# Four adjacency layers on one core: where last-pass norms sit inside a score step, a first map split in two, and where layer 1's first weights lie

## The chip, the cores and the metric

The kernel runs on one core of one Trainium2 chip. The metric is the device time of one execution in microseconds (us), less being better. A core has TensorE (PE, matrix products and transposes into PSUM), VectorE (DVE), ScalarE (ACT), GpSimd (POOL) and SyncE (SP, which here issues DMAs). Each engine takes its own instructions in order and waits on semaphores for the others.

## The reference

The input x is 128 batches x 64 nodes x 256 channels, adj is 64 x 64, all float32. Four layers follow each other, each of the form `x = layernorm(x + layer(x))`.

```
layer 0: two graph convolutions relu(adj @ (h W + b)), then LSTMs over windows of 1, 2, 3 and 4 nodes
layer 1: agg = A_hat @ x;  h = relu(batchnorm(agg W1.T + b1));  out = batchnorm(h W2.T + b2)
layer 2: Xq = x W_lin.T;  Xv = x W_val.T                 (4 heads)
         e[edge, head] = a . leaky_relu(Xq[src] + Xq[dst], 0.2) + log(adj[src, dst])
         attn = softmax of e over the edges of one src;   Y = sum over edges of attn * Xv[dst];   Y W_out.T
layer 3: U = eigenvectors of the normalized Laplacian of adj;  U relu((U.T x) W1 + b1) W2 + b2
```

The change touches the start of layer 1 and the place where layer 1's end and layer 2's beginning run side by side.

## The kernel before

The activations stay in one SBUF tile `X` of 128 partitions x 64 tiles x 256 channels (two batches per tile). The tile framework reorders what the source issues: it lists each engine's instructions by its own costs, so the order on an engine is not the order of the source. Where the source forces an order it does so by hand: `in_order(eng, on)` keeps what is issued inside it behind the last instruction of that engine so far, and `after(ins, those)` adds a dependency.

**Layer 1, first pass** (lines 1735 to 1753). Over 16 blocks `q` of four tiles: store the block (`xd`, an SP DMA), aggregate on PE (L1742), copy to `at` on ACT (L1744), multiply by `w1` (L1748, 8 matmuls), take statistics on DVE (`st1`, L1749) and copy out on ACT (L1750). Pieces of an eigenvalue solver (`pump`) run on DVE beside it. `w1` is loaded by an SP DMA (L1703) into a tile of pool `la`, which closes after this pass and lies above pool `lw`, in which `w2`, `vec1`, `vec2` and `st1` lie at the bottom of that side of memory. What a tile's memory held before decides how early it can be filled: here it is memory of layer 0's LSTM.

**Layer 1, second pass** multiplies by `w2` (L1796) and leaves the result in `Y` with statistics; then scale and shift of the second batchnorm are worked out.

**The last pass of layer 1** (`last_pass`) is a generator of 32 halves `h`, two tiles each, with two stops per half. In the first, PE transposes `y` (L1836) and DVE adds the result to `X` (L1234) and takes row statistics (L1237, L1238), all inside `ln.add`. In the second, ACT makes the next `y` (L1827, two instructions) and, for some `h`, `ln.flush` works out `1/sqrt` (DVE L1212, ACT L1214, DVE L1215 to L1218, L1249) and ACT normalizes each tile of the group (L1253). The condition `h % 2 or not h` flushes h = 0, h = 1, and then pairs {2,3}, {4,5} and so on to {30,31}.

**Layer 2's scores** (`scores`) go over 32 pairs of tiles `k`. `transposed(k)` transposes a pair (PE L1919, DVE copy L1921 to `xT`); `maps(k)` multiplies it by the query and value weights side by side, 512 columns in one PSUM bank per tile (L1930), ACT copies the first 256 columns to `xq` (L1932) and the others to `xv` (L1933), and SP stores `xv`. A step has two halves `c`: four score products `l` (L1956, traced as eight records), four copies to `xs` on ACT (L1963), four leaky relus on DVE (L1964), and the products `sc` of the half before (L1907). After `c = 0` comes `maps(k + 1)`, after `c = 1` comes `transposed(k + 2)`. The source makes the products `l` of a half wait for all ACT copies issued since the last half (the list `taken`), which includes the two `xq` copies of `maps`. PSUM tiles for `transposed`, `maps` and the last pass come from one pool of two banks (tag `m`); `xs` has six buffers.

**How they interleave.** `beside[0]` is the last pass, and every half of a score step calls `next(beside[0])` twice. So a step `k` takes two halves of the last pass, h = 3 + 2k in its first half and h = 4 + 2k in its second. Steps 0 to 14 run that way; later ones run with layer 2's softmax and values.

On the engines PE's order in a step is: maps, transposes of an even `y`, `l` (c = 1), `sc`, transposes of X, transposes of an odd `y`, `l` (c = 0 of the next step), `sc`, maps. Each `y` stands just ahead of an `l`.

Of the kernel before, what the change touches and what calls it, by code (L numbers as in the profile page):

```python
# [7 lines left out]
F32 = mybir.dt.float32  # L8
# [8 lines left out]
D = 256  # L17
P = 128
# [1241 lines left out]
def tile_adj_resnorm(ctx: ExitStack, tc: tile.TileContext, I: dict, out: bass.AP, layers: int = 4):  # L1260
    nc = tc.nc
    v, s, te = nc.vector, nc.scalar, nc.tensor
# [13 lines left out]
    kio = lambda w: w.rearrange("(k p) f -> p k f", p=P)  # L1276
# [202 lines left out]
    with tc.tile_pool(name="lw", bufs=1) as lw, tc.tile_pool(  # L1479
        name="l0c", bufs=1  # L1480
    ) as lc, tc.tile_pool(name="l0p", bufs=2, space=PSUM) as pp, tc.tile_pool(
        name="l0r", bufs=1, space=PSUM
# [27 lines left out]
        ps = pp.tile([P, 512], F32, tag="ps", name="ps")  # L1510
# [4 lines left out]
        ps = pp.tile([P, 512], F32, tag="ps", name="ps")  # L1515
        te.matmul(ps[:, :1], bda, ones[:, 0:1], start=True, stop=True)
        v.tensor_copy(rs, ps[:, :1])
        ps = pp.tile([P, 512], F32, tag="ps", name="ps")
# [4 lines left out]
        ln = Norm(nc, hn, X, 8)  # L1523
# [166 lines left out]
    lw, sm = own2(only1, name="l1w", bufs=1), own2(only1, name="l1s", bufs=2)  # L1690
    pass1 = ExitStack()
    la = own2(pass1, name="l1a", bufs=2)
    pp = own1(only1, name="l1p", bufs=7, space=PSUM)

    def lload(name, shape, src, eng=nc.sync):
        t = lw.tile(shape, F32, tag=name, name=name)
        eng.dma_start(t, src)
        return t

    NQ = NT // 4  # L1700
    Y = [ly.tile([P, 2, 512], F32, tag=f"Y{q}", name="Y") for q in range(NQ)]
    w1 = la.tile([P, 2, 512], F32, tag="w1", name="w1", bufs=1)
    nc.sync.dma_start(w1, kio(I["W1T"]))  # L1703
    w2 = lload("w2", [P, 4, D], kio(I["W2T"]))
    vec1 = lload("vec1", [P, 3, 4], I["vec1"], s)
    vec2 = lload("vec2", [P, 3, 2], I["vec2"], s)
    st1 = lw.tile([P, 4, NQ, 6], F32, tag="st1", name="st1")
    st2 = lw.tile([P, 2, NQ, 6], F32, tag="st2", name="st2")
    xd = [dram.tile([P, 4, D], F32, tag=f"xd{q}", name=f"xd{q}") for q in range(NQ)]

# [17 lines left out]
    def xq(q):  # L1728
        return X[:, q * 4 : q * 4 + 4, :]

    def first(q, c):

        return Y[q][:, c, :] if c < 2 else xq(q).rearrange("p j d -> p (j d)")[:, (c - 2) * 512 : (c - 1) * 512]

    back = residual(NT // TG - 1, H, pp, "ps")
    for q in range(NQ):
        nc.sync.dma_start(xd[q], xq(q))
        at = la.tile([P, 2, 512], F32, tag="at", name="at")
        for k in range(2):
            ps = pp.tile([P, 512], F32, tag="ps", name="ps")  # L1740
            for j in range(4):
                te.matmul(ps[:, j * P : (j + 1) * P], X[:, q * 4 + j, k * P : (k + 1) * P], bdah,  # L1742
                          start=True, stop=True)
            s.copy(at[:, k, :], ps)  # L1744
        for c in range(4):
            ps = pp.tile([P, 512], F32, tag="ps", name="ps")
# [40 lines left out]
    for q in range(NQ):  # L1787
        h = sm.tile([P, 4, 512], F32, tag="h", name="h")
# [24 lines left out]
    @contextmanager  # L1813
    def in_order(eng, on):

        last = next((i for i in reversed(nc.cur_bb.bb.instructions) if i.engine == eng.engine), None) if on else None
        with tc.issue_after(last) if last is not None else nullcontext():
            yield

    def last_pass():  # L1820

        ln = Norm(nc, sy, X, 8, act=True)

        def normed(h):
            y = sy.tile([P, 2, 2 * P], F32, tag="y", name="y")
            for c in range(2):
                s.activation(y[:, c, :], Y[h // 2][:, c, h % 2 * 2 * P : (h % 2 + 1) * 2 * P], AF.Identity,  # L1827
                             bias=sh2[:, c : c + 1], scale=sc2[:, c : c + 1])
            return y

        y = normed(0)
        for h in range(2 * NQ):
            ps = pp.tile([P, 512], F32, tag="m", name="m")
            for i in range(2):
                for c in range(2):
                    te.transpose(ps[:, i * D + c * P : i * D + (c + 1) * P], y[:, c, i * P : (i + 1) * P], ident)  # L1836
            ln.add(2 * h, ps, 2)
            yield
            with in_order(s, h < 4):
                if h < 2 * NQ - 1:  # L1840
                    y = normed(h + 1)
            with in_order(s, h < 4):
                if h % 2 or not h:
                    ln.flush()
            yield

# [9 lines left out]
    with ExitStack() as l2:  # L1856
# [3 lines left out]
        pp = own1(l2, name="l2p", bufs=2, space=PSUM)  # L1860
        sx = own1(scoring, name="l2x", bufs=2, side="right")
# [9 lines left out]
        wqv = lt.tile([P, 2, 2 * D], F32, tag="wqv", name="wqv")  # L1871
# [16 lines left out]
        taken, late = [], []  # L1888
        beside = [iter(())]
        es, soft = [[], []], []  # L1890

        def after(ins, those, how=mybir.DependencyClass.Sync):
            for i in those:
                tc.add_manual_dep(ins.ins, i.ins.name, mybir.DependencyInfo(how, mybir.DependencyReason.DATA),
                                  reason="together")

        def products():

            k, c, xs, ready = late.pop()
            half, u_ = divmod(k, HU)  # L1900
            if u_ == 0 and c == 0:
                sc[half] = [pc.tile([P, 512], F32, tag="sc", name="sc") for _ in range(2)]
            mms = []
            for b in range(2):
                for i in range(2):
                    q = 32 * (2 * b + i)
                    mms.append(te.matmul(sc[half][c][q : q + 32, :], az[:, c, HU - 1 - u_ : 3 * HU - 1 - u_],  # L1907
                                         xs[b, i], start=(u_ == 0), stop=(u_ == HU - 1)))
            after(mms[0], ready)
            if u_ == HU - 1 and c == 1:  # L1910
                next(soft[half])
            return mms[0]

        def transposed(k):

            ps = pp.tile([P, 512], F32, tag="m", name="m")
            for i in range(2):
                for c in range(2):
                    te.transpose(ps[:, i * D + c * P : i * D + (c + 1) * P], X[:, 2 * k + i, c * P : (c + 1) * P], ident)  # L1919
            xT = sx.tile([P, 2, 2, P], F32, tag="xT", name="xT", bufs=1)  # L1920
            v.tensor_copy(xT.rearrange("p i c n -> p (i c n)"), ps)  # L1921
            return xT

        def maps(k, xT):

            xq, xv = [], sx.tile([P, 2, D], F32, tag="xv", name="xv")
            for i in range(2):
                ps = pp.tile([P, 512], F32, tag="m", name="m")
                for c in range(2):
                    te.matmul(ps, xT[:, i, c, :], wqv[:, c, :], start=(c == 0), stop=(c == 1))  # L1930
                xq.append(sx.tile([P, D], F32, tag="xq", name="xq", bufs=4))
                taken.append(s.copy(xq[i], ps[:, :D]))  # L1932
                s.copy(xv[:, i, :], ps[:, D:])  # L1933
            nc.sync.dma_start(xvd[k], xv)
            return xq

        def scores():


            K = NT // 2  # L1940
            xT = transposed(0)
            xq = maps(0, xT)
            next(beside[0])
            xT = transposed(1)
            next(beside[0])


            four = [(b, i) for i in range(2) for b in range(2)]
            for k in range(K):
                xn = None  # L1950
                for c in range(2):
                    xs, pl = {}, [pg.tile([P, 2, 512], F32, tag="l", name="l") for _ in range(2)]
                    mms = []
                    for b, i in four:
                        r = slice(b * N, (b + 1) * N)
                        mms.append(te.matmul(pl[i][:, b, :], xq[i][r, c * P : (c + 1) * P], GG[r, :], start=True, stop=True))  # L1956
                    after(mms[0], taken)
                    del taken[:]
                    next(beside[0], None)
                    ready = []  # L1960
                    for b, i in four:
                        x = xs[b, i] = sx.tile([P, E], F32, tag="xs", name="xs", bufs=6)
                        taken.append(s.copy(x, pl[i][:, b, :]))  # L1963
                        ready.append(v.scalar_tensor_tensor(x, x, 0.2, x, ALU.mult, ALU.max))  # L1964
                    if late:
                        after(products(), mms[-1:], mybir.DependencyClass.NoSync)
                    late.append((k, c, xs, ready))
                    if c == 0 and k < K - 1:
                        xn = maps(k + 1, xT)
                    if c == 1 and k < K - 2:  # L1970
                        xT = transposed(k + 2)
                    next(beside[0], None)
                xq = xn
                if k == K - 1:
                    products()
                yield
# [98 lines left out]
        lw, sm = own1(valuing, name="l2w", bufs=1), own1(valuing, name="l2s", bufs=2)  # L2075
        ln = Norm(nc, sm, X, 4, act=True)
# [16 lines left out]
        with tc.tile_pool(name="l3w", bufs=1) as l3w, tc.tile_pool(name="l3s", bufs=2) as s3, tc.tile_pool(  # L2093
            name="l3p", bufs=6, space=PSUM
        ) as p3:
            bank = lambda: p3.tile([P, 512], F32, tag="ps", name="ps")
            w1 = l3w.tile([P, 2, P], F32, tag="w31", name="w31")
# [23 lines left out]
            ag, h, uh = {}, {}, {}  # L2121
# [117 lines left out]
```

## Time and profile before

| what | value |
|---|---|
| median of 3 runs | 2429.41 us (2428.41 to 2432.4) |
| the profiled execution's own time | 2431.46 us |
| its span, first to last instruction | 2429.7 us |
| busy share of the span: PE, DVE, ACT | 94%, 75%, 40% |
| from 1515 to 1671 us (first pass of layer 1) | PE busy 149.12 of 156 |
| from 1901.15 to 1913.67 us (one score step with last-pass work) | 12.52 long, PE busy 11.06, DVE 9.53, ACT 9.49 |
| from 2067.27 to 2077.46 us (one score step without it) | 10.19 long, PE busy 10.17 |

The profile shows one execution. "Idle before" is the time in which an engine had nothing, and the name behind the arrow is what ended that. PEclk is the share of TensorE's full clock that was granted. A row such as `PE L1956 MATMUL l<-edge_s,xq ... x8` is eight merged records of source line 1956 that write `l` and read `edge_s` and `xq`; the first two numbers are start and length in us.

### The profile page before, as it was taken

The page shows a single profiled execution, that of the slowest core. Times are in us where ns is not written, and L with a number is a line of the kernel's source. Part 1 is how long each engine was busy: PE and PEld are TensorE (multiplying, and loading weights), DVE is VectorE, ACT ScalarE, POOL GpSimd, SP SyncE. Part 2 cuts the span into 40 slices and gives each one's busy share as a digit, 9 for nine tenths or more (in the row PEclk, how much of TensorE's full clock was granted, in tenths as well). Part 3 has the DMA queues.
Part 4 walks back from the last instruction along what each step waited for, and adds up shares of the span by engine and source line. Part 5 has one row for each costly group of instructions (what it writes and reads, how often), then busy time and mean ns, then how long its engine had stood idle before and what let it go on. Part 6 is the DMA issues. An engine that isn't in the chain of part 4 may idle for free. (4 is left out here: it accounts for less than half of the span.)

```text
span 2429.7 us, 29499 instructions
## 1 busy us (share of the span) xinstructions
PE 2289.1 (94%) x9016; PEld 1225.0 (50%) x9016; DVE 1817.8 (75%) x8355; ACT 974.1 (40%) x1751; POOL 77.4 (3%) x118
## 2 busy tenths in 40 slices
PE   7999999999999999999999999999988889899797
PEld 5544654444564544665444644554433333246786
DVE  4666766677887888878888888687957778457577
ACT  2333222242333243332333222334437765456575
POOL 0000000000000000000000000000000000002331
PEclk9999999999999999999999999999989999999899
DMA  6000000100100000100001000012210000511622
GB/s 216 18 18 35 1 35 1 35 18 18 53 1 35 35 18 22 49 35 1 35 35 52 1 27 1 27 49 104 78 40 27 22 22 24 98 36 48 135 88 75
DMA packets 59861, 101.26 MB, mean 42 GB/s; under 512 B 5136, under 2 KB 40080, under 8 KB 59440
## 3 DMA queue, kind: packets, MB, share of 16 engines
q1 hardware_dynamic: 54624, 88.83, 11.5%
q0 software_dynamic: 3216, 10.21, 1.4%
q8 instruction: 72, 1.18, 0.2%
q14 instruction: 93, 0.76, 0.1%
q10 hardware_dynamic: 1856, 0.28, 0.1%
HBM read 67.84 MB, written 31.46 MB: 41 GB/s over the span
## 5 line engine op out<-in xcount | busy, mean ns | idle before, releaser
L1590 PE MATMUL pq<-H,wi 128*128 128x512 f32 (+1 forms) x2016 | 836.3, 547 | 6.0 <-DVE H L1619 4.0
L1596 ACT ACTIVATE gate<-pq,bl 128x512 f32<-128x512 f32 (+1 forms) x504 | 317.3, 634 | 791.0 <-PE pq L1594 647.0
L1590 PEld LDWEIGHTS pq<-H,wi 128*128 128x128 f32 x2016 | 371.9, 191 | 330.9 <-issue 256.2
L1594 PE MATMUL pq<-lh,wh 128*128 128x512 f32 (+1 forms) x1152 | 481.8, 534 | 16.1 <-DVE lh L1614 14.4
L1594 PEld LDWEIGHTS pq<-lh,wh 128*128 128x128 f32 x1152 | 213.1, 190 | 213.4 <-issue 128.3
L1964 DVE SCALAR_TENSOR_TENSOR xs<-xs 128x512 f32<-128x512 f32 x256 | 165.2, 680 | 88.7 <-ACT xs L1963 88.2
L1956 PE MATMUL l<-edge_s,xq 64*128 64x512 f32 x512 | 135.7, 624 | 36.2 <-ACT xq L1932 19.9
L1963 ACT COPY xs<-l 128x512 f32<-128x512 f32 x256 | 136.8, 587 | 73.6 <-PE l L1956 39.0
L1612 ACT ACTIVATE gate<-lc 128x512 f32<-128x512 f32 (+1 forms) x144 | 83.5, 580 | 166.9 <-DVE lc L1608 81.1
L1930 PE MATMUL m<-wqv,xT 128*128 128x512 f32 x256 | 124.6, 624 | 0.8 <-DVE xT L1921 0.8
L1748 PE MATMUL ps<-at,w 128*128 128x512 f32 x256 | 116.9, 608 | 6.9 <-DMA w<-in_W1T_dram 5.9
L1796 PE MATMUL ps<-h,w 128*128 128x512 f32 x256 | 114.9, 607 | 4.1 <-ACT h L1790 4.1
L1253 ACT ACTIVATE X<-X,ln_sh,ln_rs 128x256 f32<-128x256 f32 x192 | 101.0, 591 | 30.7 <-DVE ln_sh L1249 24.9
L1237 DVE BATCH_NORM_STATS2 ln_st<-X 128x6 f32<-128x256 f32 x256 | 98.7, 415 | 2.3
L142 DVE COPY AQR<-eps 64x192 f32<-64x192 f32 (+1 forms) x125 | 35.0, 280 | 80.9 <-PE eps L148 80.8
L1956 PEld LDWEIGHTS l<-edge_s,xq 64*128 64x128 f32 x512 | 46.2, 188 | 88.8 <-issue 32.6
L1930 PEld LDWEIGHTS m<-wqv,xT 128*128 128x128 f32 x256 | 46.5, 195 | 78.6 <-issue 58.3
L1796 PEld LDWEIGHTS ps<-h,w 128*128 128x128 f32 x256 | 48.8, 194 | 64.0 <-issue 52.3
L1748 PEld LDWEIGHTS ps<-at,w 128*128 128x128 f32 x256 | 47.4, 193 | 62.8 <-issue 53.7
L1610 DVE TENSOR_TENSOR gate<-gate 128x512 f32<-128x512 f32 (+1 forms) x72 | 43.4, 603 | 45.7 <-ACT gate L1596 45.2
L1907 PE MATMUL sc<-xs,az 128*32 128x512 f32 x512 | 69.0, 611 | 4.6 <-DVE xs L1964 4.6
L1550 PE MATMUL ps<-wg,h 128*128 128x256 f32 x256 | 65.4, 394 | 5.9 <-DVE h L1541 5.5
(558 smaller groups left out, 3196.4 us busy)
## 6 DMA issues: line engine op xcount, KB each, us to landing
wi<-in_WihT_dram SPq DMA_DIRECT2D x16, 1024.0 KB, 4.8
wh<-in_WhhT_dram SPq DMA_DIRECT2D x12, 1024.0 KB, 6.6
X<-in_x_dram SPq DMA_DIRECT2D x16, 512.0 KB, 8.9
xd<-X SPq DMA_DIRECT2D x16, 512.0 KB, 2.6
X<-xd SPq DMA_DIRECT2D x16, 512.0 KB, 3.2
xv<-xv SPq DMA_DIRECT2D x32, 256.0 KB, 2.0
xr<-xv POOLq DMA_DIRECT2D x32, 256.0 KB, 2.9
M<-attn_d SPq DMA_DIRECT2D x16, 512.0 KB, 11.5
```

Source lines behind the costliest of these rows:

```text
L1237: nc.vector.bn_stats(st, self.X[:, k, :])
L1253: nc.scalar.activation(x, x, AF.Identity, bias=sh[:, k : k + 1], scale=rs[:, k : k + 1])
L1590: te.matmul(ps, wi[:, kk, o * P : (o + 1) * P], at(kk, k), start=(kk == 0), stop=(k == 0 and kk == 1))
L1594: te.matmul(ps, wh[:, kk, o * P : (o + 1) * P], hst[:, kk, :M], start=False, stop=(kk == 1))
L1596: s.activation(gates[gt][:, c, :M], ps, AF.Tanh if gt == 2 else AF.Sigmoid, bias=bl[:, p - 1, o : o + 1])
L1612: s.activation(g[2], cs, AF.Tanh)
L1748: te.matmul(ps, w1[:, k, c * P : (c + 1) * P], at[:, k, :], start=(k == 0), stop=(k == 1))
L1796: te.matmul(ys[c], w2[:, k, c * P : (c + 1) * P], h[:, k, :], start=(k == 2), stop=(k == 1))
L1930: te.matmul(ps, xT[:, i, c, :], wqv[:, c, :], start=(c == 0), stop=(c == 1))
L1956: mms.append(te.matmul(pl[i][:, b, :], xq[i][r, c * P : (c + 1) * P], GG[r, :], start=True, stop=True))
L1963: taken.append(s.copy(x, pl[i][:, b, :]))
L1964: ready.append(v.scalar_tensor_tensor(x, x, 0.2, x, ALU.mult, ALU.max))
```

## The change

1. `w1` moves from pool `la` to pool `lw`, as that pool's first tile, ahead of `w2`; its DMA is issued ahead of w2's. `st1` moves from `lw` to `la`.
2. In the last pass the flush condition becomes `h < 3 or h % 2 == 0 or h == 2 * NQ - 1`: h = 0, 1 and 2 alone, then {3,4}, {5,6} and so on to {29,30}, and 31 alone. For h < 3 DVE's additions and flushes are kept in order on DVE as well, and the forced order on ACT goes one half further.
3. `maps(0)` is made `apart`: the query columns of both tiles come first, each followed by its `xq` copy, and then the value columns of both.
4. The second half of h = 2 (its `normed` and flush) is issued ahead of `transposed(1)` instead of behind it.

What the two programs' instruction orders show: PE's order differs only up to step 1, where all four `l` of step 0 now stand together behind the transposes of pair 1, and two groups of `y` transposes stand behind an `l` instead of ahead of it. On ACT, in every step up to 14, before: `xq xv`, three normalizations, `xq xv`, one normalization, `y y`, `xs xs xs xs`, `y y`, `xs xs`, the square root, `xs xs`. After: `xq xv xq xv`, `y y`, `xs xs`, the square root, `xs xs`, four normalizations, `xs xs`, `y y`, `xs xs`. On SP only the two weight loads swap.

```diff
-    w1 = la.tile([P, 2, 512], F32, tag="w1", name="w1", bufs=1)
-    nc.sync.dma_start(w1, kio(I["W1T"]))
+    w1 = lload("w1", [P, 2, 512], kio(I["W1T"]))
     w2 = lload("w2", [P, 4, D], kio(I["W2T"]))
...
-    st1 = lw.tile([P, 4, NQ, 6], F32, tag="st1", name="st1")
+    st1 = la.tile([P, 4, NQ, 6], F32, tag="st1", name="st1", bufs=1)
...
-            ln.add(2 * h, ps, 2)
+            with in_order(v, h < 3):
+                ln.add(2 * h, ps, 2)
             yield
-            with in_order(s, h < 4):
+            with in_order(s, h < 5):
                 if h < 2 * NQ - 1:
                     y = normed(h + 1)
-            with in_order(s, h < 4):
-                if h % 2 or not h:
+            with in_order(s, h < 5), in_order(v, h < 3):
+                if h < 3 or h % 2 == 0 or h == 2 * NQ - 1:
                     ln.flush()
             yield
...
-        def maps(k, xT):
+        def maps(k, xT, apart=False):
 
             xq, xv = [], sx.tile([P, 2, D], F32, tag="xv", name="xv")
+            pss = [pp.tile([P, 512], F32, tag="m", name="m") for _ in range(2)]
+
+            def product(i, cols):
+                for c in range(2):
+                    te.matmul(pss[i][:, cols], xT[:, i, c, :], wqv[:, c, cols], start=(c == 0), stop=(c == 1))
+
+            def first(i):
+                xq.append(sx.tile([P, D], F32, tag="xq", name="xq", bufs=4))
+                taken.append(s.copy(xq[i], pss[i][:, :D]))
+
+            if apart:
+                for i in range(2):
+                    product(i, slice(0, D))
+                    first(i)
             for i in range(2):
-                ps = pp.tile([P, 512], F32, tag="m", name="m")
-                for c in range(2):
-                    te.matmul(ps, xT[:, i, c, :], wqv[:, c, :], start=(c == 0), stop=(c == 1))
-                xq.append(sx.tile([P, D], F32, tag="xq", name="xq", bufs=4))
-                taken.append(s.copy(xq[i], ps[:, :D]))
-                s.copy(xv[:, i, :], ps[:, D:])
+                product(i, slice(D, 2 * D) if apart else slice(0, 2 * D))
+                if not apart:
+                    first(i)
+                s.copy(xv[:, i, :], pss[i][:, D:])
             nc.sync.dma_start(xvd[k], xv)
             return xq
...
             xT = transposed(0)
-            xq = maps(0, xT)
+            xq = maps(0, xT, True)
+            next(beside[0])
             next(beside[0])
             xT = transposed(1)
-            next(beside[0])
```

## The prediction

> **What bounds the kernel now.** The page comes first: PE is busy for 94% of the span, and the rows of its products say which stretches have idle time. Then the timeline of PE alone over two score steps, the same of ACT, the timeline around the first product with `w1`, and the busy times of windows.
>
> ```profile
> PE 2289.1 (94%) x9016; PEld 1225.0 (50%) x9016; DVE 1817.8 (75%) x8355; ACT 974.1 (40%) x1751; POOL 77.4 (3%) x118
> L1956 PE MATMUL l<-edge_s,xq 64*128 64x512 f32 x512 | 135.7, 624 | 36.2 <-ACT xq L1932 19.9
> L1748 PE MATMUL ps<-at,w 128*128 128x512 f32 x256 | 116.9, 608 | 6.9 <-DMA w<-in_W1T_dram 5.9
> ```
>
> Two waits stand out: 19.9 us before `l` that end with an `xq` copy, and 5.9 us before the first product with `w1`.
>
> ```profile
> 1901.64 0.60 PE L1836 MATMUL m<-ident,y 128*128 128x128 f32 x4
> 1902.36 1.99 PE L1956 MATMUL l<-edge_s,xq 64*128 64x512 f32 x8
> 1904.28 1.06 PE L1907 MATMUL sc<-xs,az 128*32 128x512 f32 x8
> 1905.27 3.70 PE L1930 MATMUL m<-wqv,xT 128*128 128x512 f32 x8
> 1908.81 0.60 PE L1836 MATMUL m<-ident,y 128*128 128x128 f32 x4
> 1910.75 1.99 PE L1956 MATMUL l<-edge_s,xq 64*128 64x512 f32 x8 [1.34 <-ACT xq L1932]
> 1912.67 1.07 PE L1907 MATMUL sc<-xs,az 128*32 128x512 f32 x8
> 1913.67 0.66 PE L1919 MATMUL m<-ident,X 128*128 128x128 f32 x4
> 1914.16 0.60 PE L1836 MATMUL m<-ident,y 128*128 128x128 f32 x4
> 1914.88 1.99 PE L1956 MATMUL l<-edge_s,xq 64*128 64x512 f32 x8
> ```
>
> A step is 12.52 us (from `l` at 1902.36 to `l` at 1914.88), and PE has one gap in it, 1.34 us, always before the `l` of the second half. ACT says why:
>
> ```profile
> 1907.61 0.39 ACT L1932 COPY xq<-m 128x256 f32<-128x256 f32 x1
> 1907.88 0.40 ACT L1933 COPY xv<-m 128x256 f32<-128x256 f32 x1
> 1908.87 1.58 ACT L1253 ACTIVATE X<-X,ln_sh,ln_rs 128x256 f32<-128x256 f32 x3 [0.59 <-DVE ln_sh L1249]
> 1910.36 0.35 ACT L1932 COPY xq<-m 128x256 f32<-128x256 f32 x1
> ```
>
> The second `xq` copy stands behind three normalizations, which themselves wait for DVE. And at the start of layer 1:
>
> ```profile
> 1519.79 0.37 SPq L1703 DMA_DIRECT2D w<-in_W1T_dram  x1
> 1519.82 1.07 ACT L1744 COPY at<-ps 128x512 f32<-128x512 f32 x2 [0.81 <-DVE H L1619]
> 1523.33 9.03 PE L1748 MATMUL ps<-at,w 128*128 128x512 f32 x16 [5.91 <-DMA w<-in_W1T_dram]
> ```
>
> The weight load is issued only at 1519.79, after layer 0's last DVE write; SP has stood at it for 93 us.
>
> **Part 1, `w1`.** In the changed program the load stands where w2's stood, issued at 1426.35 in the trace, with the same kind of wait (a DVE instruction two later). It lands some 90 us early. PE then waits for the first `at` copy, which still waits for the last DVE write: 1519.82 + 0.58 (one copy) = 1520.40, so PE starts at about 1520.45 instead of 1523.33: **2.9 us**. The clock belongs to it. Here the row and a rule part ways. The granted clock is 0.5 from 1520.4 to 1527.2, and 2.56 us of idle before 901.86 and before 2028.38 were each followed by 3.4 us at 0.5 (from 902.6 and 2029.0). The Trainium skill, "TensorE: Matmul & The Clock Gate", section "HAM oscillation — how this bites in real kernels", says to avoid idle gaps over about 3.4 us; by that the remaining gap of 3.03 us keeps the full clock, which would save the (1527.2 - 1523.33)/2 = 1.9 us lost now as well, 4.8 in all. The rows are nearer: the drop comes, and lasts 3.4 us instead of 6.8. PE then loses (1523.8 - 1520.45)/2 = 1.7 us instead of 1.9. I take 2.9 + 0.2 = **3.1 us**, 2.9 and 4.8 as ends. It passes on whole: in this pass PE is busy 149.12 of 156 us, and DVE and ACT wait for the same products (7.39 and 6.96 us). Behind the load on SP stand w2, one issue later and needed at 1675, and stores of blocks that layer 0's norms release later anyway. POOL's clearing of `zero` still waits for the pass. All of this costs nothing.
>
> **Part 2, the steady step.** PE's own work from maps to maps, read off the timeline start to start: maps to y 3.54, y to `l` 0.60, `l` to `sc` 1.92, to X's transposes 1.00, to y 0.49, to `l` 0.72, to `sc` 1.92, to maps 0.99: 11.18 us, the 12.52 less the gap. Independently, a step without the last pass is 10.19, and two groups of y transposes at 0.49 make 11.17. Does the new ACT order let PE keep that? With the maps at 0:
>
> - second `xq`: the maps' second bank is ready 3.63 after their start (1816.40 to 1820.03, where PE ended the wait), copied by 4.00; `l` could start at 4.14. No gap; 0.1 to spare.
> - norms: y transposes at 3.54, the addition 0.64 later, then 0.72, 0.67 and 0.3 for statistics: the square root's input at 5.8. Its place on ACT, between the two `xs` pairs, is at 6.35 (`l` + 1.16 + 1.05): 0.55 to spare. The chain of small operations runs behind two leaky relus on DVE to 8.1; four normalizations follow the second `xs` pair, 8.3 to 10.35 (2.08 by their row).
> - the next `l` (8.27) waits for the second `xs` pair: at `l` + 3.01, as now, since these copies wait for `sc` to free `xs`. Unchanged.
> - the `xs` copies of that `l`, ready at 9.45, start at 10.35, then y, then the second pair to 13.4. That is 2.2 into the next step; the first `xq` is ready at 1.92, the second at 3.63. Hidden, 0.7 to spare.
> - `sc` at 10.19 needs DVE's last leaky relu, now behind the norm chain and the copy of `xT`: 9.9. 0.3 to spare.
>
> ACT's and DVE's work per step (9.49 and 9.53 us busy) is below 11.18, so neither becomes the bound. I take 11.2 to 11.3, a gain of 1.3. From the `l` of step 2 (1848.13) to that of step 13 (1985.92) lie 11 steps: **14.3 us**. Step 14 has two normalizations left ahead of the second `xq` instead of three (tile pair 31 alone): 1.35 becomes about 0.75, **0.6 us**. The added group is six small DVE operations (1.0 us) and one 0.2 us square root; DVE's idle time in the step covers them.
>
> **Part 3, steps 0 to 2.** From 1797.94, where the last pass starts, by the same durations: the first norm no longer alternates with h = 1 on DVE, so its square root's input comes at 1801.07 instead of 1801.89 and the maps start at 1805.1 instead of 1805.93. A rule speaks against splitting them: the Trainium skill, "PSUM — Partial Sum Buffer", section "PSUM bank collisions raise a hardware error", allows no ACT read beside a PE write in one bank, even of other columns, and the program waits accordingly: a tile's value columns start after its `xq` copy. At half clock a half product lasts 1.7 us and the copy is done 0.8 us after it, while the other tile's half runs; only the second tile can wait, some 0.1 us. The four extra weight loads cost between nothing (streams follow each other) and 4 x (2 x 379 - 592) = 0.66 us, by the medians of L1550 (128x256) and L1930; I take nothing, since weight loads overlap here. All of `l` ends at 1814.5 instead of 1815.97; the next one moves from 1820.46 to 1819.5, since the add of h = 3 still holds the second bank. The next (1826.85 now) stands behind `xs` copies that follow a square root, four y and four normalizations on ACT; with those gone it starts at 1824.1. The four normalizations come one half later and take some back: 1835.32 becomes 1833.6, and from there the new period applies, so 1848.13 becomes 1844.8: **3.3 us**, between 1 and 6. The xv store is later by one copy; its reader comes much later.
>
> **Sum.** 3.1 + 3.3 + 14.3 + 0.6 = 21.3 us. The profiled execution took 2431.46, 1.76 more than its span, so it would take 2410.2; it lies 2.05 above the median of the three runs, 2429.41, so 2408.1 is the forecast. What follows the scores (softmax, fetch of the attention table, values) starts from them and shifts as a whole.
>
> **Rivals.**
>
> - *A new small wait in each step.* One of the margins above (0.1 for `xq`, 0.3 for `sc`) is short, and about half of 1.3 comes back as another gap. For it: four dependencies are within 0.6 us. Against: none is missed on the rows' numbers. 11 x 0.65 + 7 = 14 us: 2415. Chance 0.17.
> - *Only the steps gain.* The start is held by the half clock (13.7 us of it from 1796.9) and part 3 gives nothing: 18 us, 2411, inside the main case; with a lost window of clock as well (1.7 us), 2413. Chance 0.10.
> - *More than the sum.* The clock stays full at 1520 (+1.7) and the start gains 6: 25.7 us, 2403.7. Chance 0.10.
> - *Slower.* The square root sits on ACT between two `xs` pairs, in order, with its input coming from the transposes just before. If that input is late by d, the second pair, the next `l` and the step are late by d - 0.55. Before, this wait (1.95 us ahead of L1214) lay where PE had other work. It eats the step's gain at d = 1.9 and the other 7 us too at about d = 2.5; at d = 3 a step costs 1.1 more than now: 12 x 1.1 - 6.4 = 7 us slower, 2436. For it: ACT has waited for exactly this input in every step. Against: y transposes come 2.3 us before the slot. Chance 0.06.
> - *No change*: that the reordering is not made is excluded by the program's order; the gains would have to cancel. Chance 0.03.
>
> The main case has 0.54. A measurement of this kernel tells about 0.2% (4.9 us) from no change. Faster by more than that: 0.54 + 0.17 + 0.10 + 0.10 = 0.91; same 0.03; slower 0.06. The range 2402 to 2417 takes in the main case, the small wait and the bounds of part 1 and part 3.
>
> **What would show it.** Right: no wait for `w1`, its first product at 1520.4 and half clock for 3.4 us; score steps of 11.2 to 11.3 us with no gap before the second `l`; `l` of step 14 some 21 us earlier. Wrong: a step above 11.8 with a gap that ends with `xs`, `sc` or the square root; gains in the steps that are lost after 2000 us.

## The result, and the profile after

The changed kernel takes 2408.2 us (median of 4 runs, 2406.92 to 2408.46), the kernel before, beside it, 2430.08 (4 runs, 2428.41 to 2432.4). The ratio is 0.9908, 95% interval 0.9891 to 0.9925: 21.9 us less, where 21.3 were forecast. The profiled execution took 2408.46 us, with a span of 2406.7.

The page, rows for PE as a whole, for `l` and for the products with `w1` (busy time, mean ns of one, idle time ahead and what ended most of it):

```profile
PE 2289.4 (95%) x9024; PEld 1227.6 (51%) x9024; DVE 1818.3 (76%) x8361; ACT 974.4 (40%) x1752; POOL 76.6 (3%) x118
L1968 PE MATMUL l<-edge_s,xq 64*128 64x512 f32 x512 | 134.6, 624 | 18.6 <-ACT xs L1975 11.5
L1747 PE MATMUL ps<-at,w 128*128 128x512 f32 x256 | 118.0, 613 | 4.0 <-ACT at L1743 3.5
```

PE's busy time is what it was (2289.4 and 2289.1 us): the gain is idle time. 17.6 us of it stood ahead of `l`, and the largest releaser there is no longer `xq`. The idle time ahead of `w1` is down to 4.0 us, and a copy to `at` ends it instead of the DMA.

PE's timeline over two halves of a score step:

```profile
1906.34 0.60 PE L1835 MATMUL m<-ident,y 128*128 128x128 f32 x4
1906.96 1.99 PE L1968 MATMUL l<-edge_s,xq 64*128 64x512 f32 x8
...
1911.09 1.99 PE L1968 MATMUL l<-edge_s,xq 64*128 64x512 f32 x8
1913.01 1.07 PE L1907 MATMUL sc<-xs,az 128*32 128x512 f32 x8
1914.00 3.70 PE L1931 MATMUL m<-wqv,xT 128*128 128x512 f32 x8
1917.54 0.60 PE L1835 MATMUL m<-ident,y 128*128 128x128 f32 x4
```

The transposes of an even `y` at 1906.34 and at 1917.54 are one step apart: 11.20 us, with no bracket for idle time in any of the rows. From the second half's `l` of step 2 (1839.75) to that of step 13 (1962.98) lie 123.23 us, 11 times 11.20; before it was 137.79. ACT in the same stretch:

```profile
1909.10 0.22 ACT L1214 ACTIVATE is_s<-is_t 128x4 f32<-128x4 f32 x1
1909.96 1.07 ACT L1975 COPY xs<-l 128x512 f32<-128x512 f32 x2 [0.65 <-PE sc L1907]
1911.00 2.08 ACT L1253 ACTIVATE X<-X,ln_sh,ln_rs 128x256 f32<-128x256 f32 x4
1912.98 1.04 ACT L1975 COPY xs<-l 128x512 f32<-128x512 f32 x2
...
1916.03 0.37 ACT L1935 COPY xq<-m 128x256 f32<-128x256 f32 x1
1916.29 0.38 ACT L1945 COPY xv<-m 128x256 f32<-128x256 f32 x1
1917.74 0.37 ACT L1935 COPY xq<-m 128x256 f32<-128x256 f32 x1 [1.07 <-PE m L1931]
```

The four normalizations stand together, far ahead of the `xq` copies, and wait for nothing. The second `xq` copy now waits for PE: ACT has been idle for 1.07 us when the maps' second bank is ready. The square root (1909.10) does not wait either. DVE's two rows that bear on the margins of the prediction are these, the input of the square root and the leaky relus ahead of the `sc` at 1913.01:

```profile
1908.71 0.17 DVE L1212 TENSOR_SCALAR is_t<-ln_mv 128x4 f32<-128x4 f32 x1
...
1911.48 1.28 DVE L1976 SCALAR_TENSOR_TENSOR xs<-xs 128x512 f32<-128x512 f32 x2
```

The start of layer 1, PE's timeline, and then the busy times of four windows with the granted clock (PE, PEld, DVE, ACT, POOL, then PEclk):

```profile
1519.58 6.25 PE L1747 MATMUL ps<-at,w 128*128 128x512 f32 x7 [3.04 <-ACT at L1743]
```

```profile
1515.40:1518.80 3.40, 1.14 (x11) 0.95 (x9) 2.61 (x4) 1.16 (x2) 0.00 (x0) 1.00 0.05 3
1518.80:1522.20 3.40, 2.62 (x3) 1.17 (x4) 0.05 (x1) 1.07 (x2) 0.00 (x0) 0.50 0.00 0
1522.20:1525.60 3.40, 3.40 (x5) 1.33 (x4) 0.70 (x1) 0.59 (x1) 0.00 (x0) 0.50 0.00 0
1525.60:1529.00 3.40, 3.40 (x9) 1.52 (x8) 1.40 (x2) 0.85 (x2) 0.00 (x0) 1.00 0.00 0
```

The wait for the weights is gone and 3.04 us for the `at` copy remain. The clock dropped to 0.5 all the same, for 6.8 us, as long as before.

The start of the scores, PE's timeline:

```profile
1801.29 5.78 PE L1931 MATMUL m<-wqv,xT 128*128 128x256 f32 x16 [0.78 <-DVE xT L1921]
...
1808.12 1.99 PE L1968 MATMUL l<-edge_s,xq 64*128 64x512 f32 x8
...
1814.98 1.99 PE L1968 MATMUL l<-edge_s,xq 64*128 64x512 f32 x8 [0.46 <-ACT xq L1935]
...
1819.69 1.99 PE L1968 MATMUL l<-edge_s,xq 64*128 64x512 f32 x8 [0.56 <-ACT xs L1975]
...
1828.55 1.99 PE L1968 MATMUL l<-edge_s,xq 64*128 64x512 f32 x8 [0.59 <-ACT xq L1935]
```

To see what each part is worth, the two runs are cut at points that both have. The first is the end of PE's last product ahead of `w1` (an aggregation of layer 1's first block), where the idle time ahead of `w1` begins (1519.58 - 3.04).

| stretch, us | before | after | less by | forecast |
|---|---|---|---|---|
| start to PE's last product ahead of `w1` | 1517.42 | 1516.54 | 0.88 | 0 |
| from there to the last pass's first transposes | 280.52 | 277.54 | 2.98 | 3.1 |
| from there to the second `l` of step 2 | 50.19 | 45.67 | 4.52 | 3.3 |
| from there to the second `l` of step 13 | 137.79 | 123.23 | 14.56 | 14.3 |
| from there to the second `l` of step 14 | 12.52 | 12.37 | 0.15 | 0.6 |
| the rest of the span | 431.24 | 431.31 | -0.07 | 0 |

The effects add up to 22.2 us, against 21.9 between the medians. The first row is taken for no effect: PE's order is the same there, and this point lies anywhere between 1514.7 and 1520.0 us in the other runs below. Half a microsecond of the third row is not the edit's either: it comes from where the clock's half-speed stretch fell, as the kernel with the first maps in one piece shows below.

### The profile page after: what moved, and what is told of

Same layout as the page of the kernel before. It is cut to its first block, busy times and chain, and to the rows that moved or that the text cites. A ratio compares the mean times of both kernels' runs of the same rounds, so it can differ in the third digit from the quotient of the medians.

```text
span 2406.7 us, 29522 instructions
## 1 busy us (share of the span) xinstructions
PE 2289.4 (95%) x9024; PEld 1227.6 (51%) x9024; DVE 1818.3 (76%) x8361; ACT 974.4 (40%) x1752; POOL 76.6 (3%) x118
## 5 line engine op out<-in xcount | busy, mean ns | idle before, releaser
L1594 PE MATMUL pq<-lh,wh 128*128 128x512 f32 (+1 forms) x1152 | 482.8, 535 | 16.0 <-DVE lh L1614 14.3
L1931 PE MATMUL m<-wqv,xT 128*128 128x512 f32 (+1 forms) x264 | 124.6, 610 | 0.9 <-DVE xT L1921 0.8
L1619 DVE TENSOR_TENSOR H<-gate 128x512 f32<-128x512 f32 (+1 forms) x72 | 46.8, 650 | 32.2 <-ACT gate L1612 26.8
```

The costliest lines, as they stand in the source:

```text
L1594: te.matmul(ps, wh[:, kk, o * P : (o + 1) * P], hst[:, kk, :M], start=False, stop=(kk == 1))
L1931: te.matmul(pss[i][:, cols], xT[:, i, c, :], wqv[:, c, cols], start=(c == 0), stop=(c == 1))
```

## Experiments: which edit brings what

Four kernels take the change apart. **The weights alone**, put into the kernel before:

```diff
-    w1 = la.tile([P, 2, 512], F32, tag="w1", name="w1", bufs=1)
-    nc.sync.dma_start(w1, kio(I["W1T"]))
+    w1 = lload("w1", [P, 2, 512], kio(I["W1T"]))
...
-    st1 = lw.tile([P, 4, NQ, 6], F32, tag="st1", name="st1")
+    st1 = la.tile([P, 4, NQ, 6], F32, tag="st1", name="st1", bufs=1)
```

> The kernel before with one part of the change: w1 loaded where the changed program loads it, st1 moved for it. If the parts add up: PE starts the first w1 product at once after the first at copy (gap of about 3.0 us in place of 5.9), the score steps stay at 12.52 us, and the whole comes 1.8 to 3.1 us below the kernel before (3.1 by the prediction, 1.8 by what the changed kernel's trace shows up to the end of this pass: the clock stays at half for 6.8 us all the same). Rival: the other parts' shift of phase, not w1, is what made the second pass of layer 1 shorter by 1.15 us in the changed kernel; then it is 1.8 here. If that 1.15 us belongs to w1's start (the same clock window, met earlier), it is 2.9 to 3.0 at the start of the last pass.

2428.09 us against 2431.53 for the kernel before, ratio 0.9992 (0.9983 to 1.0). Its PE timeline at the start of layer 1 and in a score step:

```profile
1517.77 4.63 PE L1747 MATMUL ps<-at,w 128*128 128x512 f32 x5 [3.02 <-ACT at L1743]
```

```profile
1903.37 0.60 PE L1835 MATMUL m<-ident,y 128*128 128x128 f32 x4
1905.32 1.99 PE L1955 MATMUL l<-edge_s,xq 64*128 64x512 f32 x8 [1.35 <-ACT xq L1931]
```

The gap is 3.02 us instead of 5.91, and the steps keep their 1.35. From PE's last product ahead of `w1` to the last pass it is 277.46 us, 3.06 less than before and the same as in the changed kernel (277.54), so the other parts have no share in the 2.98 of the table: the expectation's 2.9 to 3.0 holds. The times cannot tell 1.8 from 3.0, nor from nothing: by the ratio's interval it is 0 to 4 us less. The trace does.

**The flush condition alone**, in the kernel before:

```diff
-                if h % 2 or not h:
+                if h < 3 or h % 2 == 0 or h == 2 * NQ - 1:
                     ln.flush()
```

> The kernel before with the condition of the flush alone (norms flushed in the second half of a step). By my theory the order on ACT is the whole gain of the steps: the 1.34 us gap ahead of the second half's l is gone, steps of 11.20 us, 11 x 1.32 = 14.5 us below the kernel before by step 13, and between 13 and 16 at the end, since the start keeps the old order of its parts. Rival: the start's changes are needed for it (the norms' pairs would meet another step of DVE's or ACT's queue), so that a gap of some 0.6 us stays in each step and the gain is about 7 us.

2413.48 us, ratio 0.9928 (0.9914 to 0.9941), 17.5 us less.

```profile
1901.79 1.99 PE L1956 MATMUL l<-edge_s,xq 64*128 64x512 f32 x8
...
1912.99 1.99 PE L1956 MATMUL l<-edge_s,xq 64*128 64x512 f32 x8
```

Steps of 11.20 us with no gap: one condition carries the whole of the steps' gain, and the rival (0.6 us left in each step) is out. It helps the start too, which the 13 to 16 us that I gave for it left out: from the last pass's first transposes to the second `l` of step 2 it takes 47.84 us where the kernel before takes 50.19. With the 14.56 of the steps that makes 16.9 us by the trace; the interval of the ratio (14 to 21 us) allows that.

**The start's edits alone** (the first maps in two halves, the order of the calls, the forced order on DVE and ACT), with the old condition:

```diff
-            xq = maps(0, xT)
+            xq = maps(0, xT, True)
+            next(beside[0])
             next(beside[0])
             xT = transposed(1)
-            next(beside[0])
```

> The kernel before with the third part alone: first maps in two halves with the xq halves first, both norms called before X's second transposes, the first halves in a fixed order on DVE and ACT; the condition of the flush stays. By the changed kernel's trace (8.4 us from the last pass's first transposes to the l of step 2 stand for 4.5 us less than before, 2 of which are the first two gaps ahead of l) I expect 2 to 4 us less than before, with steps of 12.52 us and the gap of 1.34 us in each. Rival: most of the 4.5 us comes from the flush, whose normalizations no longer stand ahead of the xs and xq copies of steps 0 and 1; then this is at most 1 us below the kernel before.

(The edit also has the changed kernel's `in_order` lines and its `maps` with `apart`.) 2430.81 us, ratio 0.9993 (0.9987 to 1.0), 1.7 us less, and 48.63 us to the second `l` of step 2, 1.56 less than before. That lies between what the two theories gave: both were partly right.

**The changed kernel with the first maps in one piece:**

```diff
-            xq = maps(0, xT, True)
+            xq = maps(0, xT)
```

> The changed kernel with the first maps as they were (four products of 512 columns, no halves). If the halves carry the start's gain, the first l comes 1.2 to 1.5 us later than in the changed kernel and the end by about as much. If the first l is held by the half clock and by the adds of the norms, it is within 0.4 us of the changed kernel. Steps of 11.20 us either way.

2411.39 us, ratio 0.9917 (0.9903 to 0.993). From the last pass's first transposes (1792.58) to step 0's second `l` it takes 22.32 us; in the changed kernel, with the halves, 20.90. The 1.42 us stays to the second `l` of step 2 (47.09 against 45.67), and steps are 11.20.

Not all of it belongs to the halves. The clock is at half speed for 13.7 us around this point in both, but in the changed kernel that ends 11.4 us behind the first transposes and in this one 12.5 us, as in the kernel before (12.6). The kernel with the last flush in a fixed place on ACT (a later section) has the changed kernel's start, and there the half speed also ends 12.5 us behind them. Its PE timeline, and then a window of it and one of the kernel with the maps in one piece:

```profile
1793.32 2.38 PE L1835 MATMUL m<-ident,y 128*128 128x128 f32 x8 [5.79 <-ACT y L1826]
...
1814.75 1.99 PE L1970 MATMUL l<-edge_s,xq 64*128 64x512 f32 x8 [0.46 <-ACT xq L1937]
...
1839.51 1.99 PE L1970 MATMUL l<-edge_s,xq 64*128 64x512 f32 x8
```

```profile
1792.20:1805.80 13.60, 8.82 (x25) 6.18 (x25) 7.35 (x28) 6.29 (x14) 0.00 (x0) 0.50 0.00 0
1791.50:1805.00 13.50, 8.76 (x18) 4.17 (x19) 7.32 (x28) 6.30 (x14) 0.00 (x0) 0.50 0.00 0
```

With the halves and the clock so placed it takes 21.43 us to step 0's second `l` and 46.19 to that of step 2. So with the clock in the same place the halves are worth 0.9 us, and the whole start is worth 4.0 (50.19 less 46.19); the other 0.5 of the 4.52 is the clock's position in one execution. The kernels with the flush alone and with the start's edits alone have the half speed end at 12.4 us, and their 2.35 and 1.56 add up to 3.9: neither needs the other.

The kernel with the maps in one piece also shows the clock from another side. At layer 1's start its gap is 3.01 us, but the half clock lasts one window:

```profile
1515.00:1518.40 3.40, 0.39 (x4) 0.20 (x2) 1.80 (x3) 1.35 (x3) 0.00 (x0) 1.00 0.02 1
1518.40:1521.80 3.40, 3.40 (x4) 1.40 (x5) 0.00 (x0) 0.35 (x1) 0.00 (x0) 0.50 0.00 0
1521.80:1525.20 3.40, 3.40 (x9) 1.52 (x8) 1.40 (x2) 1.17 (x2) 0.00 (x0) 1.00 0.00 0
```

The gap begins at 1515.31 here and at 1516.54 in the changed kernel. What differs is where it falls against the windows: here the window after the drop is filled by products (3.40 busy), there it still holds 0.78 us of the gap (2.62 busy), and the clock stays low for one window more.

## Experiments: the clock

**Three products of no use in the gap ahead of `w1`**, in the changed kernel:

```diff
+    def warm(n, pool=None, tag="ps"):
+        ps = pool.tile([P, 2, 512], F32, tag=tag, name=tag)[:, 0, :] if pool else pp.tile([P, 512], F32, tag=tag, name=tag)
+        for _ in range(n):
+            tc.keep_in_program_order(te.matmul(ps, w2[:, 0, :P], w2[:, 0:2, :].rearrange("p k d -> p (k d)"), start=True, stop=True))
...
             s.copy(at[:, k, :], ps)
+        if q == 0:
+            warm(3)
```

> The changed kernel with three products of no use (w2 against itself, six records of 0.457 us, 2.7 us) on PE in the 3.04 us in which it waits for the first at copy at layer 1's start. The term of the clock in my sum rests on that gap: if the gap is what halves the clock for 6.8 us at 1518.8, the clock stays full, the 16 products with w1 take 7.4 us instead of 10.1, and the kernel is 2.5 to 3 us faster. If the clock drops for another reason (the change of kind of work, or the transposes of 128 columns ahead), or if PE was held by ACT and DVE there anyway, less than 0.5 us.

2408.03 us, ratio 0.9909 (0.9893 to 0.9924): nothing that the times can show. The trace, PE's timeline and windows of the second pass:

```profile
1516.34 2.74 PE L1737 MATMUL ps<-w 128*128 128x512 f32 x6
1519.53 7.13 PE L1754 MATMUL ps<-at,w 128*128 128x512 f32 x16 [0.46 <-ACT at L1748]
```

```profile
1665.70:1669.10 3.40, 0.00 (x0) 0.00 (x0) 2.88 (x14) 0.98 (x3) 0.00 (x0) 1.00 0.96 380
1669.10:1672.50 3.40, 2.72 (x4) 1.18 (x4) 2.98 (x15) 3.40 (x6) 0.00 (x0) 0.50 0.26 89
1672.50:1675.90 3.40, 3.40 (x5) 1.35 (x4) 0.20 (x1) 2.16 (x4) 0.00 (x0) 0.50 0.63 220
```

Where it was aimed, the theory holds: the clock stays full, the 16 products take 7.13 us instead of 10.11, and the first pass, from the first `w1` product to the first `w2` product, is 150.25 us instead of 153.24. But from there to the last pass it takes 122.84 instead of 121.26. The second pass begins behind an idle stretch of 4.11 us in both kernels. In the changed one the next window is 2.98 busy and the clock returns after 3.4 us; here it is 2.72 busy and the clock stays at half for 6.8. So 1.6 of the 3.0 us are given back to the windows' position, and 1.3 remain (276.28 against 277.54 from PE's last product ahead of `w1`, not counting those of no use, to the last pass). The start of the scores takes another 0.8 back: its half speed ends 13.0 us behind the first transposes instead of 11.4, and the second `l` of step 2 comes 46.46 us behind them instead of 45.67. What is left is 0.5 us, less than the scatter of the runs.

**The same in all four idle stretches**, so that no position can take it back:

```diff
+        if q == 0:
+            warm(3)
...
     pump(5)
+    warm(4)
     for q in range(NQ):
...
+    warm(6)
     sc2, sh2 = affine("n2", st2, vec2, 2)
...
+            tc_warm(3)
             xT = transposed(0)
```

(`tc_warm` is the same with `wqv` and a bank of the pool of `l`.)

> As the kernel with products of no use ahead of the first w1 product, and the same in the three other idle stretches from there to the first scores: four ahead of layer 1's second pass (4.11 us idle), six ahead of the last pass (5.79 us) and three ahead of X's first transposes (2.87 us). If the idle time halves the clock there too, the half clock of 3.4 us at 1672.4 and of 13.7 us at 1791.8 goes, and 3 us (w1), 1.5 us (second pass) and 2.5 to 3.5 us (last pass up to the first l) are won: 7 to 8 us. Rival: in the last pass the chain of norms on DVE and ACT sets the first l, not PE's clock; then it is 4 to 5 us.

2402.42 us, ratio 0.9885 (0.987 to 0.99), about 5.6 us below the changed kernel (0.9908). No window between layer 1's start and the scores is at half clock. The first pass again gives 3.0 us (150.24), the second none (121.30 where the changed kernel has 121.26), and from the last pass's first transposes to the first `l` it is 11.18 us instead of 14.04, 2.86 less. My 7 to 8 us had 1.5 too many for the second pass. Its own products did become 1.5 us shorter (114.00 against 115.47), but the six products ahead of the last pass end late and give that back:

```profile
1784.45 5.42 PE L1737 MATMUL ps<-w 128*128 128x512 f32 x12 [2.04 <-DVE st L1807]
1789.71 1.04 PE L1844 MATMUL m<-ident,y 128*128 128x128 f32 x8
```

ACT began the four `y` instructions at 1787.61. In the changed kernel PE's transposes began 0.65 us behind ACT (1794.08 and 1793.43), so here they could have begun at 1788.26; they began 1.45 us later, since PE was still busy with work of no use.

## Experiments: room on ACT, and the last flush

**More work on ACT behind the normalizations** measures how much the new order has to spare:

```diff
                     ln.flush()
+                    if 4 <= h < 2 * NQ - 1:
+                        for _ in range(5):
+                            s.copy(sy.tile([P, D], F32, tag="junk", name="junk"), X[:, 2 * h, :])
```

> The changed kernel with five more ACT copies (128x256) behind the four normalizations of each step of scores, so some 1.4 to 1.8 us more on ACT per step. It measures the room that the new order left ahead of the second xq copy. My prediction had 0.7 us to spare: a step would become 11.2 + 0.7 to 1.1. The changed kernel's trace shows ACT idle for 1.07 us ahead of that copy: 11.2 + 0.3 to 0.7. If ACT's order does not bound the step at all (the idle time came from elsewhere), steps stay at 11.20.

2461.41 us, ratio 1.0128 (1.0113 to 1.0144): 30 us slower than the kernel before. Neither 0.7 nor 1.07 us of room explains steps of 14.5 us and more. PE's timeline, then ACT's:

```profile
1902.06 0.55 PE L1835 MATMUL m<-ident,y 128*128 128x128 f32 x3 [2.89 <-ACT xv L1948]
```

```profile
1896.92 2.07 ACT L1253 ACTIVATE X<-X,ln_sh,ln_rs 128x256 f32<-128x256 f32 x4 [1.22 <-DVE ln_sh L1249]
1898.90 1.61 ACT L1847 COPY junk<-X 128x256 f32<-128x256 f32 x5
1900.41 1.05 ACT L1978 COPY xs<-l 128x512 f32<-128x512 f32 x2
1901.37 0.37 ACT L1938 COPY xq<-m 128x256 f32<-128x256 f32 x1
```

The experiment changed two things. With the five copies the framework listed ACT in another order: the square root and the normalizations stand one `xs` pair later, the first `y` pair one later and the second one earlier, so that only one `xs` pair is left between the normalizations with their copies of no use and the `xq` copies. ACT waits 1.22 us for the norms' small operations on DVE, and the rest stands behind. The `y` transposes then wait 2.89 us for the `xv` copy that frees their bank. This step takes 14.52 us at full clock (1888.0 to 1902.5: 1.00); of the 11 steps five take 15.5 to 15.9, and in the one behind this the clock is at half from 1903.1 (0.50), so a part of the loss is the clock's. **Three copies** keep the changed kernel's order:

```diff
-                        for _ in range(5):
+                        for _ in range(3):
```

> The changed kernel with three more ACT copies (128x256) behind the four normalizations of each step of scores, in the changed kernel's own order on ACT. The five copies of the run before took 1.61 us, so three take about 0.97 us. By the 1.07 us in which ACT is idle ahead of the second xq copy, a step stays at 11.20 us; by the 0.7 us that my prediction had to spare, it becomes 11.45 to 11.5, some 3 us in all. If the 50 us of the run with five copies came from their time and not from the order that changed with them, a good part of it shows here: three fifths of it would be 30 us.

2409.28 us, ratio 0.9913 (0.9896 to 0.9929).

```profile
1903.42 1.00 ACT L1847 COPY junk<-X 128x256 f32<-128x256 f32 x3
1904.32 1.05 ACT L1978 COPY xs<-l 128x512 f32<-128x512 f32 x2
...
1908.18 0.37 ACT L1938 COPY xq<-m 128x256 f32<-128x256 f32 x1 [0.32 <-PE m L1934]
```

1.00 us more on ACT in each step, and the idle time ahead of the second `xq` copy falls from 1.07 to 0.32; the 11 steps take 123.23 us as before. (The start is 1.7 us longer, 47.37 against 45.67 to the second `l` of step 2.) The three copies put off the next `xs` pair by 0.90 us (1903.42 to 1904.32), and 0.32 was still left: the room was about 1.2 us, not 0.7. Whether the order or the time of the five copies cost their 53 us against the changed kernel is not separated; three fifths of it did not appear with three fifths of the copies, which speaks for the order.

**The last flush one half step later.** The first form only moved the call:

```diff
+            if h == 2 * NQ - 1:
+                yield
             with in_order(s, h < 5):
```

> The changed kernel with the last norm (half 31) flushed one half step later. Step 14 kept a gap of 1.20 us ahead of its second l, which ends with an xq copy behind normalizations, where my sum had 0.75. If these are the last flush's, the gap goes: step 14 takes 11.2 us instead of 12.37, 1.2 us less in all. If the gap only moves to the next half step, the end is within 0.3 us.

2411.38 us, ratio 0.9918 (0.9905 to 0.9932). Step 14 took 12.37 us and kept its gap of 1.20: ACT's order around it was the same as without the edit, so this run tells nothing of the theory. The second form puts the flush itself in order on ACT:

```diff
-            with in_order(s, h < 5), in_order(v, h < 3):
+            if h == 2 * NQ - 1:
+                yield
+            with in_order(s, h < 5 or h == 2 * NQ - 1), in_order(v, h < 3):
```

> The changed kernel with the last norm (half 31) flushed behind step 14's xq and xv copies, in a fixed place on ACT (its earlier form left ACT's order as it was). If the gap of 1.20 us ahead of step 14's second l is those two normalizations, step 14 takes 11.2 us instead of 12.37 and the kernel is 1.2 us below the changed one. If it only moves, because two normalizations now stand ahead of the next xs copies, within 0.3 us.

2409.06 us, ratio 0.9908 (0.9891 to 0.9924). ACT's timeline in step 14:

```profile
1973.52 0.37 ACT L1937 COPY xq<-m 128x256 f32<-128x256 f32 x1 [1.01 <-PE m L1933]
...
1974.05 0.22 ACT L1214 ACTIVATE is_s<-is_t 128x2 f32<-128x2 f32 x1
1975.54 1.09 ACT L1253 ACTIVATE X<-X,ln_sh,ln_rs 128x256 f32<-128x256 f32 x2 [1.27 <-DVE ln_sh L1249]
```

The normalizations now wait behind the `xq` copies instead of ahead of them. Step 14 takes 11.20 us, 1.17 less, as expected, and the step behind it does not give it back (4.83 us to its first `l` in both). The medians cannot show 1.2 us.

**Both together**, with four products of no use ahead of the last pass instead of six:

> Both together: the products of no use in the four idle stretches (four instead of six ahead of the last pass, since the six ended 1.0 us behind the moment when the first y was ready) and the last flush in its fixed place. If the parts add up: 5.7 us for the clock, 1.0 us for the shorter row and 1.2 us for the last flush, so 7 to 8 us below the changed kernel, about 0.9875 of the kernel before. If the four leave enough idle time for the clock to drop to half at the last pass, 2.9 us of it are gone again.

2402.43 us, ratio 0.9878 (0.9861 to 0.9894), the lowest ratio of all, about 7 us below the changed kernel by the ratios. The last flush brought its part in the trace (step 14 at 11.21 us). The shorter row brought nothing: in this run a window at half clock (from 1789.6) fell on it, so that four products lasted 5.40 us, and the `y` transposes began at 1794.69, again 1.5 us later than they could (ACT began `y` at 1792.54). Against the version without the last flush's edit (0.9885) it is not told apart.

## Why the prediction was right, and which terms were off

**The steady step** (14.3 forecast, 14.56 measured) was right in mechanism and size. The step is 11.20 us, the sum of PE's own work start to start gave 11.18; the old 1.34 us gap is gone; and the flush condition alone does it. The margins are in part thinner than I had them, and none is missed. The second `xq` copy ends at 1918.11, 0.06 us ahead of the next `l` at 1918.17 (0.1 forecast); the square root's input is ready at 1908.88, 0.2 us ahead of the root (0.55 forecast); the leaky relus end at 1912.76, 0.25 us ahead of `sc` (0.3 forecast). Only the room on ACT was larger, about 1.2 us instead of 0.7.

**The weights** (3.1 forecast, 2.98 measured up to the last pass). The 2.9 us of earlier start came as worked out: the gap fell from 5.91 to 3.04. The term of the clock was wrong in its parts. I had the half clock last 3.4 us where the profile shows 6.8, so the first pass gained 1.8 and not 3.1 (its first `ident,H` transposes started at 1529.52 instead of 1532.20, 2.68 less, of which 0.88 lies ahead of `w1`'s gap). That the total came out near 3.1 is luck in part: the second pass made up for it with half clock for 3.4 us instead of 6.8, 1.15 us that the sum did not have. Together the two passes are at half clock for 10.2 us in all the kernels with the early weights and no products of no use (6.8 and 3.4 in five, 3.4 and 6.8 in two) and for 13.7 us in the three with the late ones. So it hardly matters which pass has the longer stretch: from PE's last product ahead of `w1` to the last pass it is 277.3 to 277.6 us in the first and 279.9 to 280.5 in the second, a gain of 2.3 to 3.3 us. The Trainium skill, "TensorE: Matmul & The Clock Gate", section "HAM oscillation — how this bites in real kernels", warns of idle gaps over about 3.4 us, by which 3.03 us would have kept the clock. The windows decide against that: 3.04 us of idle time lowered it, and filling the gap kept it full.

**The start** (3.3 forecast, 4.52 measured) was the term most off, inside its bounds of 1 and 6. I had left the clock's half speed where it was, so the run to compare with is the one in which it ends 12.5 us behind the first transposes (the kernel with the last flush in a fixed place), and there the start gains 4.0. Measured from the last pass's first transposes: step 0's second `l` at 21.43 us, forecast 21.56 (1819.5 less 1797.94); step 1's first at 26.14, forecast 26.16; step 1's second at 34.99, forecast 35.66. In the profile after, with the clock's half speed ending earlier, all of these come 0.5 us sooner. So the forecast was good up to the last of them and 0.67 off there, where the four normalizations that "take some back" took back less: PE waited 0.40 us for `xv` and 0.59 for `xq`. The halves of the first maps ran as worked out: their row (1801.29, 5.78 us) has no idle time in it, and a tile's value columns start only when its `xq` copy has ended.

**Step 14** (0.6 forecast, 0.15 measured). I took the gap to shrink with the normalizations ahead of the second `xq` copy, from three to two, and left out what those two wait for: the square root of the last group waits 1.63 us for its statistics, the normalizations another 0.58 us for DVE, and the `xq` copy stands behind them. The gap stayed at 1.20 us; with the flush behind the `xq` copies it is gone.

**The rivals.** A new small wait per step is excluded: no row of the steady step has idle time worth naming. That only the steps gain is excluded by the start's 4.0. The gain of a full clock, given 1.7 us at layer 1's start, is 3.0 there when the gap is filled, but did not come by itself. The late square root did not come about, with 0.2 us to spare. What it would cost if it did was not tried.

## What to carry to other kernels

When an engine that is not the bound delays the bound one, look at what its short urgent copies stand behind: moving the flush by one half step, a single condition, brought 17 of the 22 us, and busy times did not change. After such a reordering compare the instruction order itself, since extra work, or a moved call, can change the order more than the time that it takes. And cost a stretch of half clock up to the next common point of both runs: a gain that shifts the program against the clock's windows may be given back in the next stretch.

## What the hardware showed beside

The granted clock changes only on a grid. In the profile after, four stretches of half clock in a row begin at 1416.4, 1518.8, 1672.4 and 1791.8 us, and the distances (102.4, 153.6, 119.4) are 30, 45 and 35 times 3.413 us, as a free-running window of 3413 ns gives it (the Trainium skill, "TensorE: Matmul & The Clock Gate", Part 1); in the other runs the grid lies elsewhere against the program. One window's work decides the next: 1.14 us of PE work in a window at full clock lowered it, and at half clock 2.98 us of work in a window raised it again where 2.72 and 2.62 did not. So the same gap of 3.0 us is followed by 3.4 us of half clock in one execution and by 6.8 in another, and before two profiles are compared to a tenth of a microsecond, their half-speed stretches have to lie in the same place.
